# A bilinear graph layer on one core: weight sums on GpSimd, first words copied to PSUM, product 3 formed like the others, and a new order

## The chip, the cores and the metric

The kernel runs on one core of a Trainium2 chip. The metric is the device time of one execution in microseconds. The core has TensorE (PE, with its weight loads listed apart as PEld), VectorE (DVE), ScalarE (ACT), GpSimd (POOL) and SyncE (SP), which here issues the transfers. Engines work side by side and wait for each other on semaphores.

## The reference, cut to what matters

```
h   = relu(layernorm(x))                           # x: 64 batches of 256 x 768, fp32
ctx = (adj  @ (h @ Wadj.T)) / deg                  # adj: 64 x 256 x 256, 0 or 1
    + (adj' @ (h @ Wrev.T)) / rdeg
    +  h @ Wself.T                                 # three 768 x 768 weights
out = x + ctx + (a small term from the 0/1 relations through Wr, Wrr)
```

Biases are zero in the inputs. The work is in the three 768 x 768 products per batch and in the two products with adj.

## The kernel before, in words

**Words.** TensorE's fast fp32 form (fp32r) doesn't keep full precision, so each operand is split into words: `word0` is the value scaled by `LOWER` and written as fp32r by ScalarE, `rest` is the value less word0 (DVE), `word2` is the rest scaled by `STEP` (ACT), and `word1` is a combination of word0 and rest (DVE). One product of a weight sum and a left operand takes 12 matmuls of 128x384.

**Products.** A bilinear scheme takes 15 products of sums of weight blocks (a "right", a sum of 256x768 thirds of the weights, loaded as `raw`) with sums of thirds of the normalized input (a "left", from `h`). They run in two sweeps over the batches: sweep 1 does products 10, 5, 2, 8, 11, 14, 3, 13 for batches 1 to 62, sweep 2 does 9, 6, 7, 15, 12, 4, 1 for the same batches and the products with adj (`agg`). Intermediates `c` go to DRAM after sweep 1 and come back in sweep 2. Batches 0 and 63 are done by `whole` with plain fp32 matmuls straight from the raw blocks (72 in program order each, two instructions apiece in the trace): batch 0 in the opening, while the words of sweep 1 are made, and batch 63 in the changeover between the sweeps, while those of sweep 2 are made.

**Where the rights come from.** `prepare(n, s, rank)` makes the words of product n. Before, the sums of raw blocks are DVE `tensor_tensor` (L539), except product 3, whose name stands in `ON_PE`: TensorE forms its sum by multiplying the raw blocks with identity and minus-identity matrices (L502, fp32), and its rest and word 1 with scaled diagonals (L507, fp32r), all inside one PSUM buffer. Words come from ACT (L551 word0, L561 word2; L516 and L521 for product 3) and DVE (L555 rest, L565 word1; L526 casts for product 3). L555 and L565 read two SBUF operands.

**What orders the work.** Every operation is recorded in a `Plan` with an engine, an estimated duration and a rank; the table `OFFSETS` is added to ranks by the kind of operation. `Plan.schedule` then lists them: each engine takes the ready operation of the lowest rank, as long as buffers of its class are free (`SLOTS`, among them 4 PSUM buffers of class Q), and an operation with `lock` waits until the other locked one (DVE sums, rest and word1, and everything on POOL) is over by the estimates. What comes out is a fixed program order for each engine.

**The rest of a batch.** x is loaded, its statistics are taken on DVE (L714 to L724), the mean and scale go through DRAM and come back as a row over all partitions (`d`, then `row`, L729 and L736), POOL centres h (L745), DVE scales and clips it (L749). POOL adds thirds (L590), ACT and DVE make the left words (L600, L607, L613, L617), TensorE multiplies (L628), ACT scales a product between its two halves (L666) and DVE or ACT reads it (L676, L685, L687). In sweep 2 a small product `rows` with `token` (L638, tiles of 32 rows) is added.

Of the kernel before, what the change touches and what calls it, by code (L numbers as in the profile page):

```python
# [10 lines left out]
F32 = mybir.dt.float32  # L11
# [6 lines left out]
P = 128  # L18
# [62 lines left out]
ON_PE = (3,)  # L81
APART = (14,)
AHEAD = 5.0
PACE = 5.0
# [26 lines left out]
    "degree@": 18.6, "degree@1": -76.25, "diagonal": 16.77, "eT": -64.36, "eps": -1.93, "eps$": 8.55,  # L111
# [1169 lines left out]
```

## Time and profile before

| | |
|---|---|
| median of 3 runs | 2477.93 us (2477.17 to 2478.81) |
| profiled execution | 2478.37 us |
| its span in the profile | 2476.5 us (1.87 us lie around it) |
| PE busy | 2449.1 us, 99% |
| DVE, ACT, POOL busy | 85%, 72%, 52% |
| granted TensorE clock | 0.999 of full (2.4 GHz) |

Busy time counts overlapping records of pipelined matmuls once; the pitch between starts of matmuls tells what one costs. A line such as `[0.42 <-DVE x L793]` says that the engine sat idle for 0.42 us before this instruction, and which instruction ended last before it could go on.

### The profile page before, as it was taken

The numbers are of one execution on the slowest core, as the hardware profiler recorded it, in microseconds if no ns is written. First come the engines' busy times: TensorE is split into PE (matmuls) and PEld (weight loads), VectorE is DVE, ScalarE is ACT, GpSimd is POOL, SyncE is SP. The second block draws the span as 40 slices with busy tenths as digits, with TensorE's granted clock in tenths as the row PEclk, the third lists the DMA queues.
The fourth block names the chain that finished last, engine by engine and source line by source line (L and its number), as shares of the span: only waits on it lengthen the run. The fifth ranks groups of instructions, "written<-read, shape, count | busy, mean of one in ns | idle before, by whom it ended". The sixth has DMA issues, their size and how long they took to land.

```text
span 2476.5 us, 43288 instructions
## 1 busy us (share of the span) xinstructions
PE 2449.1 (99%) x13858; PEld 2365.0 (95%) x13858; DVE 2096.0 (85%) x4003; ACT 1777.2 (72%) x3772; POOL 1283.1 (52%) x1138
## 2 busy tenths in 40 slices
PE   6999999999999999999999999999999999999998
PEld 4899999999999999996999999999999999999998
DVE  7887888788788878878988889888888888888987
ACT  4788888888888888886666666666666666666665
POOL 1555555555555555543555555555555555555554
PEclk9999999999999999999999999999999999999999
DMA  5677777777777777876666666666666666666664
GB/s 214 241 284 281 268 277 284 271 274 282 277 268 280 285 270 275 293 254 215 223 214 216 216 217 212 216 217 215 213 213 213 216 215 216 217 216 214 215 219 135
DMA packets 224776, 590.66 MB, mean 239 GB/s; under 512 B 25080, under 2 KB 25080, under 8 KB 224544
## 3 DMA queue, kind: packets, MB, share of 16 engines
q1 hardware_dynamic: 224544, 587.86, 69.5%
q8 instruction: 110, 1.80, 0.3%
q14 instruction: 122, 1.00, 0.1%
HBM read 364.28 MB, written 223.48 MB: 237 GB/s over the span
## 4 chain that ended last, share of the span: by engine, by line
PE 97%; DVE 1%; DMA 1%; ACT 1%; issue 0%; POOL 0%; SPq 0%; ACTq 0%; POOLq 0%
PE x L628 21%; PE y L628 21%; PE agg L944 14%; PE z L628 10%; PE w L628 10%; PE t L628 5%; PE v L628 5%; PE u L628 5%; PE whole L782 2%; PE v L638 1%; DMA raw<-in_Wself_dram 0%; PE right L502 0%; PE pt L915 0%; DMA row<-d 0%; DVE right L555 0%
## 5 line engine op out<-in xcount | busy, mean ns | idle before, releaser
L932 POOL TENSOR_TENSOR hl<-c,hl 128x768 fp32r<-128x768 f32 x256 | 474.7, 1855 | 646.3 <-ACT hl L928 470.6
L628 PE MATMUL x<-word,left 128*128 128x384 f32 x2976 | 589.3, 339 | 0.2 <-DVE c L687 0.2
L628 PE MATMUL y<-word,left 128*128 128x384 f32 x2976 | 569.3, 335 | 0.0
L628 PEld LDWEIGHTS x<-word,left 128*128 128x128 f32 x2976 | 515.2, 188 | 14.2 <-issue 11.0
L628 PEld LDWEIGHTS y<-word,left 128*128 128x128 f32 x2976 | 517.8, 188 | 5.2 <-ACT y L666 1.0
L944 PE MATMUL agg<-hl,a 128*128 128x384 f32 x2048 | 395.3, 334 | 0.0
L944 PEld LDWEIGHTS agg<-hl,a 128*128 128x128 f32 x2048 | 358.4, 188 | 0.6 <-issue 0.2
L745 POOL TENSOR_TENSOR h<-h,row 128x768 f32<-128x768 f32 x128 | 234.6, 1855 | 177.5 <-DMA row<-d 132.2
L628 PE MATMUL z<-word,left 128*128 128x384 f32 x1488 | 299.3, 335 | 0.7 <-DVE x L793 0.4
L628 PE MATMUL w<-word,left 128*128 128x384 f32 x1488 | 298.2, 334 | 0.2 <-ACT w L666 0.2
L666 ACT ACTIVATE x<-x 128x768 f32<-128x768 f32 x248 | 191.8, 794 | 137.1 <-PE x L628 136.4
L628 PEld LDWEIGHTS z<-word,left 128*128 128x128 f32 x1488 | 258.7, 188 | 4.5 <-DVE x L793 0.7
L628 PEld LDWEIGHTS w<-word,left 128*128 128x128 f32 x1488 | 261.3, 188 | 0.8 <-ACT w L666 0.5
L955 DVE SCALAR_TENSOR_TENSOR c<-agg,rd,c 128x768 f32<-128x768 f32 x252 | 255.2, 1013 | 7.1 <-PE agg L944 3.9
L928 ACT ACTIVATE hl<-c 128x768 fp32r<-128x768 f32 x256 | 215.2, 841 | 30.9 <-DVE c L685 25.0
L666 ACT ACTIVATE y<-y 128x768 f32<-128x768 f32 x248 | 197.1, 795 | 41.5 <-PE y L628 41.4
L722 POOL TENSOR_TENSOR cols<-cols,half 128x2 f32<-128x2 f32 x64 | 83.0, 1296 | 252.7 <-DVE cols L721 252.7
L617 DVE SCALAR_TENSOR_TENSOR left<-left,top 128x256 fp32r<-128x256 f32 x496 | 199.5, 413 | 6.4
L685 DVE TENSOR_TENSOR c<-c,v 128x768 f32<-128x768 f32 x124 | 117.5, 947 | 102.0 <-PE v L628 101.1
L617 DVE SCALAR_TENSOR_TENSOR left<-left 128x256 fp32r<-128x256 f32 x434 | 203.3, 490 | 0.1
L607 ACT ACTIVATE top<-left 128x256 f32<-128x256 f32 x496 | 181.0, 383 | 6.2 <-DVE left L617 2.0
L676 ACT ACTIVATE c<-y 128x768 f32<-128x768 f32 x124 | 101.1, 815 | 70.0 <-PE y L628 69.9
(136 smaller groups left out, 4308.3 us busy)
## 6 DMA issues: line engine op xcount, KB each, us to landing
c<-kept SPq DMA_DIRECT2D x316, 384.0 KB
kept<-c SPq DMA_DIRECT2D x252, 384.0 KB
x<-in_x_dram SPq DMA_DIRECT2D x128, 384.0 KB
h<-in_x_t_dram SPq DMA_DIRECT2D x128, 384.0 KB
out_dram<-c SPq DMA_DIRECT2D x126, 384.0 KB
kept_h<-h SPq DMA_DIRECT2D x124, 384.0 KB
h<-kept_h SPq DMA_DIRECT2D x124, 384.0 KB
adj<-in_adj_dram SPq DMA_DIRECT2D x64, 512.0 KB
```

The lines of the kernel that those rows point to most:

```text
L607: lambda: nc.scalar.activation(view(top), t(w)[:, 0].bitcast(F32), AF.Copy),
L617: lambda: nc.vector.scalar_tensor_tensor(t(w)[:, 2], t(w)[:, 1].bitcast(F32), -STEP, first(), op0=ALU.mult, op1=ALU.add), s == 1,
L628: nc.tensor.matmul(t(q)[:, half, : H // 2], t(w)[:, lw, f, :], t(r[rw])[:, f, ts(half, H // 2)], start=start and i == 0 and f == 0, stop=s ...
L666: lambda: nc.scalar.activation(view(), view(), AF.Copy, scale=scale),
L676: lambda o=o, sign=sign: nc.scalar.activation(t(o).rearrange("p (k n) -> p k n", k=2), view(), AF.Copy, scale=sign * (1.0 if value_last el ...
L685: emit = lambda to=to, op=op: nc.vector.tensor_tensor(to(), to(), view(), op=op)
L722: pool(0.7, r - 21.5, f"pow {b}", [col], [col], lambda: nc.gpsimd.tensor_tensor(var(), var(), v["half"], op=ALU.pow))
L745: lambda h=h, one=one: nc.gpsimd.tensor_tensor(t(h), t(h), one(0), op=ALU.subtract),
L928: lambda: nc.scalar.activation(t(pair)[:, 0], t(o), AF.Copy, scale=LOWER),
L932: lambda: nc.gpsimd.tensor_tensor(t(pair)[:, 1], t(o), t(pair)[:, 0].bitcast(F32), op=ALU.subtract),
L944: nc.tensor.matmul(t(q)[:, half, : H // 2], t(s["a"])[:, c, k, ts(ic, P)], t(pairs[c])[:, part, ts(half, H // 2)], start=(c == 0 and part ...
L955: lambda q=q, to=to, ic=ic: nc.vector.scalar_tensor_tensor(to(), t(q)[:, :, : H // 2], t(rd)[:, ic, k : k + 1], to(), op0=ALU.mult, op1=AL ...
```

## The change

1. Product 3 is formed like the others: `ON_PE`, the diagonals and the whole branch of `prepare` for it are gone.
2. Sums of raw blocks move from DVE to POOL `tensor_tensor` (L488).
3. After word0, ACT copies it into a PSUM buffer of class Q (L507); rest (L511) and word1 (L521) read this copy, so each has one PSUM operand, and they are no longer locked against POOL.
4. The PSUM buffer held back for product 3's sums can serve as a Q buffer in the opening too.
5. `schedule` widens its look-ahead when nothing else can go on, and `OFFSETS` is a new table, so the order of all engines is new.

```diff
-ON_PE = (3,)
 OFFSETS = {
-    "a0+a1+b0+b1": 8.69, "a0+a1+b0+b1$1": -94.46, "a0+a1+b0+b1@1": -28.72, "a0+a2": 6.59, "a0+a2$1": 6.18,
...
-                    if e != "PE" and steps and o.rank > steps[-1].rank + PACE:
+                    if e != "PE" and steps and o.rank > steps[-1].rank + pace:
...
+            if not events and pace < 1000.0:
+                pace *= 2.0
+                continue
+            pace = PACE
...
-        if n in ON_PE:
-            minus, small = diagonal(s, -1.0, rank - 6.0), diagonal(s, -1.0 / STEP, rank - 6.0)
...
-                                nc.tensor.matmul(
-                                    view(), one, r[f][1]()[:, ts(h, H // 2)], start=i == 0, stop=i == len(parts) - 1
-                                )
...
-            return
...
-                    dve(
-                        on_dve(H), rank - 3.0 + 0.1 * f, f"right{n}", reads, [h],
-                        lambda h=h, f=f, r=r, op=op, src=src: nc.vector.tensor_tensor(t(h), src(), r[f][1](), op=op), True,
-                    )
...
+                pool(
+                    on_pool(H), rank - 3.0 + 0.1 * f, f"right{n}", reads, [h],
+                    lambda h=h, f=f, r=r, op=op, src=src: nc.gpsimd.tensor_tensor(t(h), src(), r[f][1](), op=op),
+                )
...
+            q = plan.buf("Q", [P, 2, 512], F32, f"copy{n}_{f}")
...
+            act(
+                in_place(H), rank - 1.8 + 0.1 * f, f"copy of {n}", [(w[0], f)], [q],
+                lambda f=f, view=view: nc.scalar.activation(view(), two(t(w[0])[:, f, :].bitcast(F32)), AF.Copy),
+            )
             dve(
-                on_dve(H), rank - 1.5 + 0.1 * f, f"rest of {n}", reads + [(w[0], f)], [h],
-                lambda f=f, h=h, src=src: nc.vector.scalar_tensor_tensor(
-                    t(h), src(), sign, t(w[0])[:, f, :].bitcast(F32), op0=ALU.mult, op1=ALU.subtract
-                ), True,
+                on_dve(H), rank - 1.5 + 0.1 * f, f"rest of {n}", reads + [q], [h],
+                lambda h=h, src=src, view=view: nc.vector.scalar_tensor_tensor(
+                    two(t(h)), two(src()), sign, view(), op0=ALU.mult, op1=ALU.subtract
+                ),
             )
```

By engine, sums go from 26 on DVE (16 in the opening) to 30 on POOL (20 in the opening); rest and word1 from 28 to 30 each; ACT gains 30 copies; TensorE loses 20 matmuls in program order, all in the opening.

TensorE in the opening, before (`whole` is batch 0 of plain fp32 matmuls, `right` is product 3's sum in PSUM):

```order
2 L782 MATMUL whole_0_647<-raw_0_607,h_0_605 128x384 x4
3 L502 MATMUL right_00_675<-raw_0_639,ident 128x384
4 L502 MATMUL right_00_675<-raw_0_641,diagonal-1.0_0_652 128x384
5 L502 MATMUL right_00_675<-raw_0_634,diagonal-1.0_0_652 128x384
6 L502 MATMUL right_01_687<-raw_0_639,ident 128x384
7 L502 MATMUL right_01_687<-raw_0_641,diagonal-1.0_0_652 128x384
8 L502 MATMUL right_01_687<-raw_0_634,diagonal-1.0_0_652 128x384
9 L782 MATMUL whole_0_647<-raw_0_644,h_0_605 128x384 x4
10 L782 MATMUL whole_0_711<-raw_0_641,h_0_636 128x384 x4
11 L507 MATMUL right_00_675<-word_0_718,diagonal-1.0_0_652 128x384
```

and of the change, at the end of the same stretch:

```order
14 L738 MATMUL whole_0_832<-raw_0_709,h_0_605 128x384 x4
15 L738 MATMUL whole_0_874<-raw_0_726,h_0_609 128x384 x4
16 L738 MATMUL whole_0_832<-raw_0_728,h_0_605 128x384 x4
17 L738 MATMUL whole_0_874<-raw_0_709,h_0_609 128x384 x4
18 L738 MATMUL whole_0_874<-raw_0_728,h_0_609 128x384 x4
19 L584 MATMUL y_1_968<-word_0_641,left_1_952 128x384 x4
20 L584 MATMUL y_1_968<-word_2_670,left_1_952 128x384 x4
```

The `whole` matmuls now follow each other without anything between them, and the first product (y of batch 1) comes right behind.

GpSimd in the opening, before (h is centred, then thirds of it are added):

```order
10 L745 TENSOR_TENSOR h_0_605<-h_0_605,row_628 128x768
11 L745 TENSOR_TENSOR h_0_636<-h_0_636,row_628 128x768
12 L722 TENSOR_TENSOR cols_89<-cols_89,half 128x2
13 L722 TENSOR_TENSOR cols_88<-cols_88,half 128x2
14 L745 TENSOR_TENSOR h_1_716<-h_1_716,row_849 128x768
15 L745 TENSOR_TENSOR h_1_694<-h_1_694,row_849 128x768
16 L590 TENSOR_TENSOR b2-a_0_1_929<-h_1_694,h_1_716 128x256
17 L590 TENSOR_TENSOR b0+b_0_1_934<-h_1_694 128x256
```

and of the change, from the 19th of the 20 sums on:

```order
31 L488 TENSOR_TENSOR right_0_849<-right_0_849,raw_0_713 128x768
32 L488 TENSOR_TENSOR right_1_861<-right_1_861,raw_0_713 128x768
33 L678 TENSOR_TENSOR cols_88<-cols_88,half 128x2
34 L701 TENSOR_TENSOR h_1_792<-h_1_792,row_841 128x768
35 L701 TENSOR_TENSOR h_1_827<-h_1_827,row_841 128x768
36 L546 TENSOR_TENSOR b2-a_0_1_938<-h_1_827,h_1_792 128x256
37 L546 TENSOR_TENSOR b0+b_0_1_941<-h_1_827 128x256
```

The 20 sums stand between the centring of batch 0 and that of batch 1.

TensorE in a period of sweep 2, before (batch 15; `rows` is the small product with tiles of 32 rows):

```order
2028 L944 MATMUL agg_14_17897<-hl_14_17781,a_17557 128x384 x4
2029 L944 MATMUL agg_14_17897<-hl_14_17858,a_17557 128x384 x4
2030 L638 MATMUL v_15_17828<-rows,token_91 128x384 x2
2031 L638 MATMUL u_15_17840<-rows,token_91 128x384 x2
2032 L628 MATMUL x_15_17738<-word_0_14161,left_15_17789 128x384 x4
2033 L628 MATMUL x_15_17738<-word_2_14175,left_15_17789 128x384 x4
```

and of the change:

```order
2008 L900 MATMUL agg_14_17935<-hl_14_17797,a_17590 128x384 x4
2009 L900 MATMUL agg_14_17935<-hl_14_17898,a_17590 128x384 x4
2010 L584 MATMUL x_15_17779<-word_0_14279,left_15_17818 128x384 x4
2011 L584 MATMUL x_15_17779<-word_2_14575,left_15_17818 128x384 x4
2012 L594 MATMUL v_15_17867<-rows,token_91 128x384 x2
2013 L594 MATMUL u_15_17880<-rows,token_91 128x384 x2
```

The four matmuls with `rows` moved behind eight of x, in each of the 62 periods.

## Rows read from the trace of the kernel before

**Rows 1.** Windows: stretch, us; then busy (x instructions) of each engine; clock, DMA, GB/s.

```profile
20.00:40.00 20.00, 20.00 (x61) 11.90 (x61) 18.13 (x22) 8.86 (x13) 1.41 (x1) 1.00 0.90 350
200.00:1020.00 820.00, 820.00 (x4722) 815.71 (x4721) 662.42 (x1477) 691.59 (x1379) 455.69 (x443) 1.00 0.77 277
1140.00:1180.00 40.00, 38.78 (x161) 27.42 (x160) 37.82 (x51) 22.39 (x49) 16.71 (x14) 1.00 0.52 189
1300.00:2400.00 1100.00, 1100.00 (x6392) 1075.13 (x6391) 977.06 (x1691) 710.97 (x1634) 578.57 (x477) 1.00 0.67 215
```

**Rows 2.** Timeline of PE in the opening: start, us, engine, line, operation.

```profile
18.93 7.20 PE L782 MATMUL whole<-raw,h 128*128 128x384 f32 x16 [18.93 <-DVE h L749]
...
26.61 1.45 PE L502 MATMUL right<-raw,diagonal-1.0_0_652 128*128 128x384 f32 x4
27.90 0.81 PE L502 MATMUL right<-raw,ident 128*128 128x384 f32 x2
...
76.09 2.16 PE L628 MATMUL y<-word,left 128*128 128x384 f32 x8
78.67 1.66 PE L628 MATMUL z<-word,left 128*128 128x384 f32 x8 [0.42 <-DVE x L793]
80.17 1.55 PE L628 MATMUL w<-word,left 128*128 128x384 f32 x8
81.56 0.68 PE L628 MATMUL y<-word,left 128*128 128x384 f32 x3
```

**Rows 3.** Groups of PE by line, 18 to 77 us: busy us, mean ns.

```profile
L502 PE MATMUL right<-raw,diagonal-1.0_0_652 128*128 128x384 f32 x16 | 5.8, 486 | 0.0
L502 PE MATMUL right<-raw,ident 128*128 128x384 f32 x8 | 3.2, 486 | 0.0
L507 PE MATMUL right<-word,diagonal-1.0_0_652 128*128 128x384 f32 x4 | 2.1, 556 | 0.0
```

**Rows 4.** Timeline of the start: issue of row, first centring on POOL.

```profile
11.26 0.35 SPq L736 DMA_DIRECT2D row<-d  x1
...
16.09 1.80 POOL L745 TENSOR_TENSOR h<-h,row 128x768 f32<-128x768 f32 x1 [8.95 <-DMA row<-d]
```

**Rows 5.** Groups of POOL: L932, L590 whole run; L745, L722 from 0 to 77 us.

```profile
L932 POOL TENSOR_TENSOR hl<-c,hl 128x768 fp32r<-128x768 f32 x256 | 474.7, 1855 | 646.3 <-ACT hl L928 470.6 <-DMA c<-in_x_dram 158.7 <-PE x L628 9.7
L745 POOL TENSOR_TENSOR h<-h,row 128x768 f32<-128x768 f32 x4 | 8.1, 2034 | 10.5 <-DMA row<-d 8.9 <-DMA h<-in_x_t_dram 1.5
L722 POOL TENSOR_TENSOR cols<-cols,half 128x2 f32<-128x2 f32 x3 | 3.4, 1120 | 39.5 <-DVE cols L721 39.5
...
L590 POOL TENSOR_TENSOR b0+b<-h 128x256 f32<-128x256 f32 x62 | 47.6, 768 | 4.5 <-DVE h L749 3.8 <-DVE line L724 0.7
```

**Rows 6.** Groups of ACT: L551 from 0 to 77 us; L666, L607 whole run.

```profile
L551 ACT ACTIVATE word<-right 128x768 fp32r<-128x768 f32 x10 | 8.1, 839 | 16.8 <-DVE right L539 16.6 <-PE whole L782 0.2
L666 ACT ACTIVATE x<-x 128x768 f32<-128x768 f32 x248 | 191.8, 794 | 137.1 <-PE x L628 136.4 <-DVE left L617 0.6
L607 ACT ACTIVATE top<-left 128x256 f32<-128x256 f32 x496 | 181.0, 383 | 6.2 <-DVE left L617 2.0 <-ACT left L600 0.3
```

**Rows 7.** DVE: sums in the opening; the read of a PSUM operand, whole run.

```profile
L539 DVE TENSOR_TENSOR right<-raw,raw 128x768 f32<-128x768 f32 x10 | 9.2, 952 | 0.2 <-DMA raw<-in_Wrev_dram 0.2
...
L685 DVE TENSOR_TENSOR c<-c,u 128x768 f32<-128x768 f32 x124 | 117.8, 950 | 0.3 <-PE u L628 0.2
```

**Rows 8.** Timeline: POOL and DVE side by side in the opening.

```profile
58.40 4.29 POOL L745 TENSOR_TENSOR h<-h,row 128x768 f32<-128x768 f32 x2
...
58.60 4.90 DVE L565 SCALAR_TENSOR_TENSOR word<-word,right 128x768 fp32r<-128x768 f32 x2
```

**Rows 9.** Waits of PEld, whole run: us in total, times, longest.

```profile
PEld v L638 <- DVE c L685: 15.0, 60, 0.3
```

**Rows 10.** Timeline of PEld: the small product in the first period of sweep 2 and in a later one.

```profile
1188.34 0.18 PEld L638 LDWEIGHTS v<-rows,token 32*128 32x128 f32 x2 [0.25 <-issue]
...
1518.19 0.18 PEld L638 LDWEIGHTS v<-rows,token 32*128 32x128 f32 x2 [0.25 <-DVE c L685]
```

More of the change, by code (lines that the diff above doesn't have):

```diff
@@ L326, in schedule @@
                 heapq.heappush(ready[o.eng], (o.rank, o.i, o))
-        events, done, now, locked, queue, out = [], 0, 0.0, 0.0, 0.0, []
+        events, done, now, locked, queue, out, pace = [], 0, 0.0, 0.0, 0.0, [], PACE
         steps = sorted((o for o in self.ops if o.eng == "PE"), key=lambda o: o.rank)[::-1]
@@ L477, in load_raw @@
         return raws[kn, s]
-    diagonals = {}
-    def diagonal(s, scale, rank):
-        if (s, scale) not in diagonals:
-            d = diagonals[s, scale] = plan.buf("S", [P, P], F32R, f"diagonal{scale}_{s}")
-            act(0.3, rank, "diagonal", [], [d], lambda: nc.scalar.activation(t(d), v["ident"], AF.Copy, scale=scale))
-        return diagonals[s, scale]
     def prepare(n, s, rank):
@@ L490, in prepare @@
         w = words[n] = [plan.buf("W", [P, 2, H], F32R, f"word{n}_{i}") for i in range(3)]
-        if n in ON_PE:
-            minus, small = diagonal(s, -1.0, rank - 6.0), diagonal(s, -1.0 / STEP, rank - 6.0)
-            for f in range(2):
-                for h in range(2):
-                    q = plan.buf("U", None, None, f"right{n}_{f}{h}", inside=hold)
-                    view = lambda q=q: t(q)[:, : H // 2]
-                    part = lambda a, f=f, h=h: t(a)[:, f, ts(h, H // 2)]
-                    def total(view=view, f=f, h=h):
-                        for i, (sign, r) in enumerate(parts):
-                            one = v["ident"] if sign == "+" else t(minus).bitcast(F32)
-                            nc.tensor.matmul(
-                                view(), one, r[f][1]()[:, ts(h, H // 2)], start=i == 0, stop=i == len(parts) - 1
-                            )
-                    def take(d, view=view, part=part):
-                        nc.tensor.matmul(view(), t(d), part(w[0]), start=False, stop=True, skip_group_check=True)
-                    at = rank + 0.2 * f + 0.1 * h
-                    key = (f, h)
-                    pe(
-                        0.17 + 0.65 * len(parts), at - 3.0, f"right of {n}", [r[f][0] for _, r in parts] + [minus], [q], total
-                    )
-                    act(
-                        in_place(H // 2), at - 2.0, f"word0 of {n}", [q], [(w[0], key)],
-                        lambda view=view, part=part: nc.scalar.activation(part(w[0]), view(), AF.Copy, scale=LOWER),
-                    )
-                    pe(0.35, at - 1.5, f"rest of {n}", [minus, (w[0], key), q], [q], lambda take=take: take(minus))
-                    act(
-                        in_place(H // 2), at - 1.0, f"word2 of {n}", [q], [(w[2], key)],
-                        lambda view=view, part=part: nc.scalar.activation(part(w[2]), view(), AF.Copy, scale=STEP),
-                    )
-                    pe(0.35, at - 0.5, f"less of {n}", [small, (w[0], key), q], [q], lambda take=take: take(small))
-                    dve(
-                        on_dve(H // 2), at - 0.3, f"word1 of {n}", [q], [(w[1], key)],
-                        lambda view=view, part=part: nc.vector.tensor_copy(part(w[1]), view()),
-                    )
-            return
@@ L531, in prepare @@
             h = halves[f]
-            if len(parts) > 1:
-                for i, (sign, r) in enumerate(parts[1:]):
-                    src = parts[0][1][f][1] if i == 0 else (lambda h=h: t(h))
-                    reads = [parts[0][1][f][0], r[f][0]] if i == 0 else [h, r[f][0]]
-                    op = ALU.add if sign == "+" else ALU.subtract
-                    dve(
-                        on_dve(H), rank - 3.0 + 0.1 * f, f"right{n}", reads, [h],
-                        lambda h=h, f=f, r=r, op=op, src=src: nc.vector.tensor_tensor(t(h), src(), r[f][1](), op=op), True,
-                    )
-                assert parts[0][0] == "+"
-        sign = -1.0 if parts[0][0] == "-" and len(parts) == 1 else 1.0
+            for i, (sign, r) in enumerate(parts[1:]):
+                src = parts[0][1][f][1] if i == 0 else (lambda h=h: t(h))
+                reads = [parts[0][1][f][0], r[f][0]] if i == 0 else [h, r[f][0]]
+                op = ALU.add if sign == "+" else ALU.subtract
+                pool(
+                    on_pool(H), rank - 3.0 + 0.1 * f, f"right{n}", reads, [h],
+                    lambda h=h, f=f, r=r, op=op, src=src: nc.gpsimd.tensor_tensor(t(h), src(), r[f][1](), op=op),
+                )
+        assert parts[0][0] == "+" or len(parts) == 1
+        sign = -1.0 if parts[0][0] == "-" else 1.0
         for f in range(2):
             h = halves[f]
+            q = plan.buf("Q", [P, 2, 512], F32, f"copy{n}_{f}")
+            two = lambda a: a.rearrange("p (k n) -> p k n", k=2)
+            view = lambda q=q: t(q)[:, :, : H // 2]
             if len(parts) > 1:
@@ L1084, in main_path @@
         psum = main.enter_context(tc.tile_pool(name="psum", bufs=1, space=bass.MemoryType.PSUM))
-        singles = ExitStack()
-        single = singles.enter_context(tc.tile_pool(name="single", bufs=1, space=bass.MemoryType.PSUM))
-        held, late = None, None
+        now, turns = ExitStack(), ["early", "single", "late"]
+        single = now.enter_context(tc.tile_pool(name=turns[0], bufs=1, space=bass.MemoryType.PSUM))
         plan = Plan(SLOTS)
@@ L1104, in main_path @@
         record(nc, plan, fixed, B, NREL)
-        for o in plan.schedule():
+        order = plan.schedule()
+        held = next(b.slot for b in plan.bufs if b.name == "hold")
+        for o in order:
             for b in o.bufs:
-                if b.name == "hold":
-                    held = b.slot
-                elif b.tile is None:
+                if b.tile is None and b.name != "hold":
                     home = {"Q": psum, "U": single, "S": small}.get(b.cls, pool)
-                    if b.cls == "Q" and b.slot == held:
-                        if late is None:
-                            singles.close()
-                            late = main.enter_context(tc.tile_pool(name="late", bufs=1, space=bass.MemoryType.PSUM))
-                        home = late
+                    if b.cls == "U" or b.cls == "Q" and b.slot == held:
+                        if (b.cls == "U") != (turns[0] == "single"):
+                            now.close()
+                            del turns[0]
+                            single = now.enter_context(tc.tile_pool(name=turns[0], bufs=1, space=bass.MemoryType.PSUM))
+                        home = single
                     b.tile = home.tile(b.shape, b.dtype, tag=f"{b.cls}{b.slot}", name=b.name)
             o.emit()
+        main.push(now)
     def general_path(sub: ExitStack):
```

22 lines of the change are left out of this document (11 added, 11 removed), and 278 rows, old and new, of the table OFFSETS.

## The prediction, made before the change was run

> **What bounds the kernel now.** I read the windows first, to see in which stages TensorE is not full [rows 1]. From 200 to 1020 us (sweep 1) and from 1300 to 2400 us (sweep 2) it is busy for all 820 and all 1100 us, with VectorE, ScalarE and GpSimd below it. In these stages only fewer or better packed matmuls can save time, and the change takes none away there. What is left is the opening, where TensorE doesn't start before 18.93 us and then works on batch 0 [rows 2], a short wait of 0.42 us at 78.67 [rows 2], and the changeover, with 1.2 us of idle PE between 1140 and 1180 us [rows 1]. So I read the timeline of PE in the opening next. The reader is to see that it is full from 18.93 to 76.09 us, that what fills it are `whole` and the 32 matmuls of product 3's sums, and that what ends its first wait is the normalized h, behind the row that comes back from DRAM at 16.09 us [rows 4].
>
> The sums are made against the profiled execution: 2478.37 us, 0.44 us above the median of 2477.93 us.
>
> **The change, part by part.**
>
> *TensorE loses product 3's sums.* 24 fp32 instructions (L502) and 8 fp32r ones (L507, four as in the row and four with the other diagonal) [rows 3]. Their means of 486 and 556 ns overlap, so I take pitches: four fp32 in 27.90 − 26.61 = 1.29 us, 0.3225 each; eight fp32r in 81.56 − 80.17 = 1.39 us, 0.174 each [rows 2]. 24 × 0.3225 + 8 × 0.174 = 7.74 + 1.39 = 9.1 us. From the other side: `whole` alone would be 7.04 us for its first 16 (from 18.93 to the first L502, which stood six pitches ahead of 27.90, at 25.97) plus 128 × 0.3225 = 41.3 us, and 57.16 − 48.3 = 8.8 us. I take 9.0, with 8.8 and 9.1 as bounds. `whole` would then end near 18.9 + 48.2 = 67.1 us.
>
> *Whether anything else is ready by 67.1 us* decides how much of this counts. The first y needs the words of product 5, made long before, and left words of batch 1, which stand behind 20 weight sums on GpSimd. The trace has no such sum on POOL. The nearest row is a 128x768 tensor_tensor with two SBUF inputs, 1855 ns over 256 in the whole run; in the opening the same form took 2034 ns [rows 5], but there it overlapped VectorE instructions that read two SBUF operands: two of L745 took 4.29 us just where two of L565 took 4.90 [rows 8]. With the copy in PSUM, L511 and L521 become like L685, whose 950 ns show no such stretching beside POOL [rows 7]. So I take 1855. The chain: centring batch 0 from 16.09, two at 1.8 to 19.7; 20 × 1.855 = 37.1, to 56.8; two pows (L722, 1.12 each) to 59.0; centring batch 1, 3.7, to 62.7; two thirds at 0.77, to 64.2; then the left words, two steps on ACT and two on DVE of the same 256 columns, each near L607's 383 ns [rows 6] and a hand-over, to about 65.9. That is 1.2 us before 67.1. The end of `whole` still decides, but narrowly.
>
> *ScalarE.* 16 copies to PSUM come in the opening. A 768-wide copy into PSUM isn't in the trace; bounds are 794 ns in place in PSUM (L666) and 839 ns from SBUF to SBUF (L551) [rows 6]. I take 0.8: 12.8 us more, less about 1.1 from product 3's parts and the diagonals. ACT was busy only 8.86 us of the 20 between 20 and 40 us [rows 1], so together 48 word instructions of about 0.8 = 38 us lie in the 46 us between 20 and 66, behind POOL's pace of one sum per 1.855 us. Hidden by `whole`; without that cover the excess over POOL's chain would show.
>
> *VectorE* loses 16 sums of 952 ns [rows 7] and four casts, and gains four instructions of about 0.95: 11 to 13 us less. It was on no path of PE but for short waits, so I count nothing for it.
>
> *The late products.* Before, the first products lost 0.42 us waiting for x [rows 2]. After, the second half of the first y waits for a scale on ACT that stands behind the copies of product 14, which themselves need a PSUM buffer that `whole` leaves late; two copies and a scale at 0.8 are 2.4 us, against 1.4 to 2.8 us of other matmuls (8 to 16 at 0.174). I count nothing, and ±1.5 us.
>
> *The start.* In SP's list one raw load (768 KB) ahead of d and row is replaced by an h (384 KB). At the 350 GB/s that the queues moved at [rows 1] 384 KB are 1.1 us. If row isn't held up by that load nothing changes. 0 to 1.1; I take 0.5.
>
> *The changeover.* Ten sums move to POOL (18.6 us at 1855), and POOL was busy 16.71 of the 40 us from 1140 on [rows 1]. PE stood idle for 1.2 us; the new order puts eight matmuls of v ahead of batch 63's last products. I take 1.0 us back, between 1.5 lost (if POOL's hl, needed by agg, comes late) and 1.5 gained.
>
> *The sweeps.* In sweep 1 the second half of product 13 moves four matmuls forward; every scale that a second half waits for keeps at least eight matmuls (1.39 us) of cover against 0.79 of a scale. In sweep 2 product 4's second half has eight instead of twelve. The moved `rows` matmuls had the largest named wait, 15.0 us over 60 periods on a DVE read [rows 9], and eight more matmuls would cover that read. But the first period shows the same 0.25 us with "issue" as its end [rows 10]: the gap is there without the DVE wait. So I count 0 for it. By the Trainium skill, page "TensorEngine Tiling (Array Packing)", section "Key Properties", changing the tiling mode drains TensorE, which fits a gap at both entries to 32-row tiles; by that rule too the sum gets nothing.
>
> Sum: 2478.4 − 9.0 − 0.5 − 1.0 = 2467.9, so **2468 us**, with its own range of 2465.5 to 2470.5 from the bounds above.
>
> **The rivals.**
>
> *A, GpSimd becomes the bound of the opening.* At the opening's own 2034 ns [rows 5] the 20 sums take 3.6 us more, the left words come at 69.5 and the first y waits 2.4 us: 2470.3. At 2145 ns, half of the 4.29 [rows 8], 5.8 us more and 4.6 us of wait: 2472.5. For it: the margin is only 1.2 us, and raw blocks may land late. Against: the PSUM copies. The Trainium skill, "GPSIMD Engine Reference", section "Engine selection", speaks against the move: elementwise work on a tile belongs on VectorE, GpSimd being about twice as slow with two inputs. The trace agrees on the ratio, 1855 against 952 ns; by the rule alone VectorE should keep the sums. That costs only where POOL ends last, which is this rival.
>
> *B, a new wait in every period of a sweep* (the other side). Product 4's scale in sweep 2 has 1.39 us for about 0.2 of waiting for the matmul's end, 0.79 of scaling and 0.1 or so to be seen: 0.3 to spare. If ACT comes to it later by more than that, for example because a left word ahead of it in ACT's list waits for a DVE read, each 0.1 us costs 62 × 0.1 = 6.2 us. From 0.17 us a period on, the gain of 10.5 is gone; at 0.25 the time is 2468 + 15.5 = 2483.4, slower. Against it: ACT is busy 711 of 1100 us in sweep 2 [rows 1], so a late ACT isn't the rule.
>
> *C, the DVE wait of `rows` is real.* If PE loses about 0.09 us a period of the 0.25 (the matmul ahead of it covers the rest), 62 × 0.09 = 5.6 us more come back: 2462.3. Rows 10 speak against it.
>
> *D, the changeover turns worse.* Hl and the sums queue on POOL, and a raw block comes late: 2 to 5 us lost instead of 1.0 gained: 2471 to 2474.
>
> **How the numbers follow.** Chances: forecast 0.62, A 0.14, B 0.09 (half of it beyond no change), C 0.07, D 0.08. The range from 2462.5 to 2473.5 holds the forecast, A, C nearly, and most of D, and leaves out about 0.15. Faster by over 0.2% (5.0 us, about what a measurement of this kernel can tell from no change) means below 2473.0: the forecast, A, C, most of D and a little of B, 0.88. Within 0.2%: 0.08. Slower: 0.04.
>
> **What would show it.** In the changed profile the `whole` group should run from 18 to 19 us for 48 us without a break, the first y should start at 66.5 to 68 with little idle before it, and L488 should read about 1.86 us. The windows of both sweeps should hold as many matmuls as before, give or take one in a thousand. If L488 reads 2.0 or more and y names POOL or the left words as what it waited for, A is right. If the wait of `rows` falls and the period with it, C is. If a wait of PE for ACT's t shows 60 times, B is. The prediction is wrong altogether if the opening shortens by 9 us and the sweeps lose it, or if the left words come well after 67 us.

## The result, and the profile after

The changed kernel takes 2503.56 us (median; 2500.62 to 2504.39) against 2478.37 us for the kernel before: ratio 1.01, 95% interval 1.0082 to 1.0117. It is **slower**, by about 25 us or 1.0%, where 10.5 us of gain were forecast. The profiled execution takes 2500.62 us, with a span of 2498.8 us and a granted clock of 0.999.

First the opening. The timeline of PE in the changed kernel answers to [rows 2]:

```profile
19.57 48.86 PE L738 MATMUL whole<-raw,h 128*128 128x384 f32 x144 [19.57 <-DVE h L705]
68.41 1.93 PE L584 MATMUL y<-word,left 128*128 128x384 f32 x8
72.54 0.96 PE L584 MATMUL y<-word,left 128*128 128x384 f32 x4 [2.20 <-ACT y L622]
73.54 1.66 PE L584 MATMUL z<-word,left 128*128 128x384 f32 x8
...
81.42 0.76 PE L584 MATMUL w<-word,left 128*128 128x384 f32 x3 [0.68 <-DVE cols L677]
```

`whole` runs as one block, and the first y comes at 68.41 instead of 76.09: 7.7 us ahead. Then TensorE waits 2.20 us for the first y's scale and 0.68 us at 81.42. The windows answer to [rows 1]:

```profile
20.00:40.00 20.00, 20.00 (x57) 11.51 (x57) 12.53 (x14) 12.20 (x16) 20.00 (x12) 1.00 0.89 340
200.00:1020.00 820.00, 820.00 (x4722) 815.64 (x4721) 657.02 (x1473) 692.60 (x1380) 455.68 (x444) 1.00 0.80 278
1140.00:1180.00 40.00, 38.67 (x172) 29.00 (x171) 35.77 (x49) 27.69 (x55) 25.93 (x21) 1.00 0.51 172
1300.00:2400.00 1100.00, 1091.43 (x6278) 1054.38 (x6278) 998.30 (x1661) 702.98 (x1609) 593.09 (x468) 1.00 0.66 211
```

Sweep 1 holds 4722 matmul records in 820 us, as before. Sweep 2 holds 6278 in 1100 us where it held 6392, at the same clock. 114 matmuls at the 0.174 us of [rows 2] are 19.8 us of work that didn't fit into these 1100 us. So the loss is in sweep 2.

The small product with `rows` stands once in each of its periods. Before, its first start is at 1188.34 [rows 10] and its last at 2456.06: 1267.7 us. After, they are at 1183.70 and 2477.03: 1293.3 us. The distances between two starts (periods, from here on) were all 20.81 to 20.85 us before, but for the first and the last. After, there are two kinds among the 61: 30 are 20.82 or 20.83, and 23 are 21.65 to 22.16, typically 21.77. The other eight are the first, the last three and four of 20.91 to 21.30. The ledger of the profiled executions: 4.6 us ahead at 1183.70, 25.6 lost between the first and the last `rows`, and the rest, 1.3, behind the last one: 22.3 us, the difference of 2500.62 and 2478.37.

The waits of the changed kernel name one release in sweep 2 which the kernel before doesn't show for PE, and for PEld once, with 0.2 us:

```profile
PEld x L584 <- DVE c L641: 17.5, 26, 0.7
...
PE x L584 <- DVE c L641: 9.1, 23, 0.4
```

Why VectorE is late is seen in the timeline of the changed kernel, by setting a short period (from 1208) beside a long one (from 1229). L573 is the second step of a left word (product 6's and 7's here, both operands in SBUF), L888 GpSimd's subtraction for the lower word of c, L641 the reads of TensorE's results:

```profile
1208.15 0.75 DVE L573 SCALAR_TENSOR_TENSOR left<-left 128x256 fp32r<-128x256 f32 x2
1208.59 2.02 POOL L888 TENSOR_TENSOR hl<-c,hl 128x768 fp32r<-128x768 f32 x1 [1.60 <-ACT hl L884]
1208.82 1.81 DVE L641 TENSOR_TENSOR c<-c,t 128x768 f32<-128x768 f32 x2
...
1229.41 2.13 POOL L888 TENSOR_TENSOR hl<-c,hl 128x768 fp32r<-128x768 f32 x1 [1.74 <-ACT hl L884]
1229.42 2.41 DVE L573 SCALAR_TENSOR_TENSOR left<-left 128x256 fp32r<-128x256 f32 x2
1231.75 1.81 DVE L641 TENSOR_TENSOR c<-c,t 128x768 f32<-128x768 f32 x2
...
1234.74 0.94 DVE L641 TENSOR_TENSOR c<-c,x 128x768 f32<-128x768 f32 x1
...
1235.73 0.97 PE L584 MATMUL x<-word,left 128*128 128x384 f32 x4 [0.40 <-DVE c L641]
```

The same two instructions take 0.75 us where GpSimd starts 0.44 us behind them, and 2.41 us where it starts 0.01 us ahead. Of the 2.41 the pair's first instruction takes 0.42 and its second 2.07, to 0.29 us behind the end of GpSimd's, which itself takes 2.13 instead of the 1.855 of [rows 5]. So by these times GpSimd's instruction came in between the two. The reads of t and x come 1.66 us later, and TensorE, whose next product is added to the buffer of x, waits for the second of them. Over sweep 2, 23 such pairs took 2.39 to 2.43 us; in 22 of them GpSimd had started 0.01 to 0.03 us ahead, in the last one 0.07 us behind. Where it started within a microsecond behind a pair that took 0.75, it was 0.44 us behind or more, 34 times. 21 of the 23 long periods hold a long pair, and the other two long pairs stand in the last periods. The two long periods without one have causes of their own: in that of 22.16 L888 holds the instruction ahead of the pair (L569, 2.09 us instead of 0.42), and in that of 21.65 ACT comes late, which is told below.

This agrees with the Trainium skill, page "SBUF — State Buffer", section "SBUF: two separate sides": of a VectorE operation with two SBUF inputs and a GpSimd operation that reads SBUF, whichever starts first holds the shared ports for its whole instruction. The rows show the hold over a whole instruction, 2.07 us against 0.42. Which of the two comes first isn't to be read from the recorded starts alone: with GpSimd's 0.01 us ahead, the pair's first instruction still ran in 0.42 us.

The timeline also shows what brings the two together. About 4.5 us earlier in the period VectorE makes another such pair, of products 1 and 9, and GpSimd adds two thirds (b1+b) for product 15. These rows are from the same short period and the same long one:

```profile
1203.83 0.76 DVE L573 SCALAR_TENSOR_TENSOR left<-left 128x256 fp32r<-128x256 f32 x2
1204.33 0.85 POOL L546 TENSOR_TENSOR b1+b<-h 128x256 f32<-128x256 f32 x1 [0.60 <-DVE left L573]
...
1224.66 1.30 DVE L573 SCALAR_TENSOR_TENSOR left<-left 128x256 fp32r<-128x256 f32 x2
1224.87 0.81 POOL L546 TENSOR_TENSOR b1+b<-h 128x256 f32<-128x256 f32 x1 [0.30 <-DVE c L641]
```

Where the addition starts 0.04 to 0.29 us behind the start of this first pair, the pair takes 1.30 us; where it starts 0.33 us behind or later, 0.75. VectorE then reaches the second pair 4.76 us behind the first instead of 4.31, and L888 starts 4.75 us behind the first in both periods: so they meet. In sweep 2 the first pair is lengthened in 25 periods, and 23 of these hold a long second pair; no other period does. When the addition starts is set by a load of h from DRAM: in 56 of 59 periods it starts 0.16 us behind the landing of a transfer that it waits for. The groups of GpSimd in sweep 2, in the changed kernel and in the one before, show that this wait is new:

```profile
L546 POOL TENSOR_TENSOR b1+b<-h 128x256 f32<-128x256 f32 x60 | 49.6, 827 | 41.4 <-DMA h<-kept_h 22.0 <-DVE left L573 7.7 <-DVE c L641 5.2
...
L590 POOL TENSOR_TENSOR b1+b<-h 128x256 f32<-128x256 f32 x60 | 44.6, 743 | 1.4 <-DMA h<-kept_h 1.0 <-DVE left L613 0.4
```

No run moved this load, so the step from it to the first pair is read from the timelines and not tested.

Before, a pair of this kind stood elsewhere. In its timeline, L932 is GpSimd's subtraction and L617 the second step of the left words:

```profile
1522.29 1.85 POOL L932 TENSOR_TENSOR hl<-c,hl 128x768 fp32r<-128x768 f32 x1 [1.46 <-ACT hl L928]
1522.64 0.94 DVE L685 TENSOR_TENSOR c<-c,v 128x768 f32<-128x768 f32 x1
1523.50 0.94 DVE L685 TENSOR_TENSOR c<-c,x 128x768 f32<-128x768 f32 x1
...
1524.37 0.76 DVE L617 SCALAR_TENSOR_TENSOR left<-left 128x256 fp32r<-128x256 f32 x1
```

Beside GpSimd's subtraction VectorE read PSUM; the left words came when it was over. The one shown met the addition behind it instead (0.76 us against 0.41), and the periods stayed at 20.8 us.

### The profile page after: what moved, and what is told of

The parts are those of the page before. It is cut to its first block, busy times and chain, and to the rows that moved or that the text cites. A ratio compares the mean times of both kernels' runs of the same rounds, so it can differ in the third digit from the quotient of the medians.

```text
span 2498.8 us, 43744 instructions
## 1 busy us (share of the span) xinstructions
PE 2455.0 (98%) x13826; PEld 2356.6 (94%) x13826; DVE 2119.7 (85%) x3977; ACT 1804.2 (72%) x3796; POOL 1359.8 (54%) x1168
## 3 DMA queue, kind: packets, MB, share of 16 engines
q8 instruction: 111, 1.82, 0.3%
## 4 chain that ended last, share of the span: by engine, by line
PE 93%; DVE 4%; DMA 1%; ACT 1%; issue 1%; POOL 0%; DVEq 0%; SPq 0%; ACTq 0%; POOLq 0%
PE x L584 21%; PE y L584 20%; PE agg L900 13%; PE w L584 10%; PE z L584 10%; PE v L584 5%; PE t L584 5%; PE u L584 5%; PE whole L738 3%; DVE c L911 1%; DVE c L641 1%; PE v L594 1%; DVE h L705 0%; DMA raw<-in_Wadj_dram 0%; DVE left L569 0%
## 5 line engine op out<-in xcount | busy, mean ns | idle before, releaser
L888 POOL TENSOR_TENSOR hl<-c,hl 128x768 fp32r<-128x768 f32 x256 | 486.7, 1902 | 390.0 <-ACT hl L884 218.5
L584 PEld LDWEIGHTS x<-word,left 128*128 128x128 f32 x2976 | 516.8, 188 | 20.5 <-DVE c L641 17.5
L900 PE MATMUL agg<-hl,a 128*128 128x384 f32 x2048 | 405.5, 339 | 1.1 <-DVE c L641 0.4
L622 ACT ACTIVATE x<-x 128x768 f32<-128x768 f32 x248 | 197.4, 796 | 187.2 <-PE x L584 181.1
L573 DVE SCALAR_TENSOR_TENSOR left<-left 128x256 fp32r<-128x256 f32 x434 | 229.8, 553 | 0.1
L573 DVE SCALAR_TENSOR_TENSOR left<-left,top 128x256 fp32r<-128x256 f32 x496 | 195.3, 414 | 6.3
L641 DVE TENSOR_TENSOR c<-c,v 128x768 f32<-128x768 f32 x124 | 118.3, 954 | 69.9 <-PE v L584 41.4
L546 POOL TENSOR_TENSOR a1+a<-h 128x256 f32<-128x256 f32 x62 | 49.3, 794 | 195.6 <-DMA h<-kept_h 128.4
```

What stands on the lines that cost most here:

```text
L573: lambda: nc.vector.scalar_tensor_tensor(t(w)[:, 2], t(w)[:, 1].bitcast(F32), -STEP, first(), op0=ALU.mult, op1=ALU.add), s == 1,
L584: nc.tensor.matmul(t(q)[:, half, : H // 2], t(w)[:, lw, f, :], t(r[rw])[:, f, ts(half, H // 2)], start=start and i == 0 and f == 0, stop=s ...
L622: lambda: nc.scalar.activation(view(), view(), AF.Copy, scale=scale),
L641: emit = lambda to=to, op=op: nc.vector.tensor_tensor(to(), to(), view(), op=op)
L888: lambda: nc.gpsimd.tensor_tensor(t(pair)[:, 1], t(o), t(pair)[:, 0].bitcast(F32), op=ALU.subtract),
L900: nc.tensor.matmul(t(q)[:, half, : H // 2], t(s["a"])[:, c, k, ts(ic, P)], t(pairs[c])[:, part, ts(half, H // 2)], start=(c == 0 and part ...
```

## The experiments

Theory 1: the loss is the collision of the pair L573 with L888 in sweep 2, which the new order of VectorE made possible. Theory 2, the rival: the pair is only where the lateness shows, and the new order of the other engines (the moved `rows` of TensorE, the other places on ACT and SyncE) or the state in which the opening leaves sweep 2 makes it; then moving the pair changes little. All kernels are the changed one with the edit shown; times of before beside them were 2478.9 to 2479.4 us.

### e1_pair_later

```diff
         order = plan.schedule()
+        for b in range(4, B - 4):
+            for n in (6, 7):
+                order = shift(order, f"left2 {n} {b}", f"read 4 {b - 1}")
```

`shift` puts the named operation behind the other in the list; only VectorE's order changes.

> The changed kernel with one thing moved: in the periods of batches 4 to 59 of sweep 2, VectorE makes the third left words of products 6 and 7 behind its two reads of t instead of ahead of them; TensorE, ScalarE, GpSimd and SyncE keep their order. Theory 1 (VectorE and GpSimd collide on SBUF: where GpSimd's subtraction for hl starts a few hundredths of a us ahead of this pair, the pair takes 2.41 us instead of 0.75, and the period 21.77 instead of 20.82): the long periods go from 56 of 62 places, and 0.9 x 24 = 22 us come back, so about 2479 us. Theory 2 (the new order of sweep 2 leaves VectorE too little room, or h and c come late from DRAM, and the pair only shows it): the long periods stay, 2498 to 2505 us.

Measured: 2484.08 us (2481.18 to 2487.33, 10 runs), 1.0023 times before (1.0013 to 1.0033). 19 of the 25 us are back. The timeline, at the same place of a period:

```profile
1522.42 1.85 POOL L898 TENSOR_TENSOR hl<-c,hl 128x768 fp32r<-128x768 f32 x1 [1.74 <-ACT hl L894]
1522.64 1.82 DVE L651 TENSOR_TENSOR c<-c,t 128x768 f32<-128x768 f32 x2
1524.38 0.75 DVE L583 SCALAR_TENSOR_TENSOR left<-left 128x256 fp32r<-128x256 f32 x2
```

The reads of PSUM run beside GpSimd at full pace (1.82 for two), and the pair behind it takes 0.75. The first pair of the period is still lengthened to 1.30 us in 24 periods of 20.83, so that meeting alone costs no time. Periods are 20.82 to 20.94 again, but for five of 21.01 to 21.51 and for the last batches, where the pair wasn't moved (21.69, 24.94 and 18.49 stand where before had 20.85, 20.84 and 21.35). Theory 1 holds for the bulk of the loss. From the first to the last `rows` 5.4 us more than before are left: 1.4 in the first period, 2.0 in the odd ones, 2.1 at the end.

### e2_sweep2_of_before

Entries of `OFFSETS` for most kinds of sweep 2 were set to those of before, two of them shown:

```diff
-"left2 6": -12.15
+"left2 6": -257.52
...
-"left2 7": -195.54
+"left2 7": -271.35
```

> The changed kernel with the old table's entries for the operations of sweep 2, so that TensorE, VectorE and GpSimd run sweep 2 in the order of before; opening, sweep 1 and changeover as in the change. If the loss lies in the order of sweep 2 (theories 1 and 2): sweep 2 takes as long as before, and what is left is the lead of 4.6 us that the change has when sweep 2 begins: 2474 us. Rival (the loss comes with the sums, the copies or the buffers, whatever the order): still above 2490 us.

Measured: 2524.65 us (2522.36 to 2526.41), 1.0189 times before: a miss. The orders of ACT and SyncE came out as a mixture of the two kernels, and TensorE waited for ACT's scale of x, which it does in neither of the two, as the waits show:

```profile
PE x L585 <- ACT x L623: 22.7, 31, 1.6
```

So it says nothing about the order of before. This mixed order costs 46 us; which of ACT's rows held the scale wasn't followed up.

### e3_no_copy and e4_sums_on_vector

These take one part of the change back in the opening and keep the order. In e3 the 30 copies to PSUM are gone, and rest and word 1 read word 0 in SBUF; in e4 the sums are on VectorE.

```diff
-                lambda f=f, view=view: nc.scalar.activation(view(), two(t(w[0])[:, f, :].bitcast(F32)), AF.Copy),
+                lambda: None,
...
-                    lambda h=h, f=f, r=r, op=op, src=src: nc.gpsimd.tensor_tensor(t(h), src(), r[f][1](), op=op),
+                    lambda h=h, f=f, r=r, op=op, src=src: nc.vector.tensor_tensor(t(h), src(), r[f][1](), op=op),
```

> The changed kernel with the same order, but without the copies of word0 into PSUM: rest and word1 read word0 from SBUF, so both their operands lie there. If GpSimd's sums and such VectorE instructions shut each other out, the 32 of them in the opening and the 20 sums take turns: a sum and two of them take 1.85 + 2 x 0.95 = 3.7 us instead of 1.9, the left words come late, and the first y starts at 80 us or later instead of 68.4. Rival (the copies buy nothing): the first y stays within 1 us of 68.4, and the 2.2 us wait behind it shrinks, since ScalarE has 12.8 us less to do.

> The changed kernel with its 30 weight sums on VectorE instead of GpSimd, everything else as it is. VectorE was busy 28.5 of the 40 us from 20 to 60; 20 sums of 0.95 are 19 us more. If VectorE then is the bound: the first y starts 4 to 8 us later than 68.4. Rival (there is room, since sums of 0.95 instead of 2.0 us make everything behind them earlier): the first y stays within 1 us of 68.4, and the move to GpSimd isn't what the opening's gain rests on.

Measured: 2534.25 us without the copies, 2519.54 us with the sums on VectorE (one run each). Without copies the first y waits 17.96 us for its left words and starts at 85.92 instead of 68.41. The groups of this opening show why:

```profile
L488 POOL TENSOR_TENSOR right<-raw,raw 128x768 f32<-128x768 f32 x12 | 29.4, 2472 | 0.6 <-DMA raw<-in_Wadj_dram 0.6
L521 DVE SCALAR_TENSOR_TENSOR word<-word,right 128x768 fp32r<-128x768 f32 x14 | 29.2, 2092 | 0.2
```

With two SBUF operands word 1 takes 2092 ns instead of the 951 of the changed kernel, and the sums beside it 2472 instead of 1896. In this order the copies are worth 17.5 us. With the sums on VectorE the timeline of PE reads:

```profile
53.14 15.72 PE L738 MATMUL whole<-raw,h 128*128 128x384 f32 x48 [1.03 <-ACT c L755]
72.89 2.93 PE L584 MATMUL y<-word,left 128*128 128x384 f32 x8 [4.02 <-ACT left L556]
```

4.5 us later than with them on GpSimd. Both parts do what the change wants of them in the opening. The rest of both losses lies mostly in the changeover, where ten sums and their words are made in the same way: the first `rows` of sweep 2 starts at 1213.17 in e3 and at 1197.03 in e4, against 1183.70. The long periods of sweep 2 stand in both.

### e5_sweep2_all_of_before

As e2, but for all kinds of sweep 2, so that all five engines have the steady order of before there. Opening, sweep 1 and changeover stay as in the change.

> As in the earlier run with sweep 2's old entries, but with all of them: in that run ScalarE and SyncE had kept a mixture of both tables' orders, and TensorE waited 20 us for ScalarE's scaled x. Now all five engines run a period of sweep 2 in the order of before, and opening, sweep 1 and changeover in the order of the change. Theory 1 (collisions of VectorE and GpSimd that the new order of sweep 2 brings): no long periods, 2478.4 minus the lead of 4 to 5 us: 2474 us. Rival (something else of the change, such as where buffers lie, makes sweep 2 longer): long periods remain, above 2480 us.

Measured: 2488.46 us (2487.9 to 2491.86), 1.0038 times before (1.0024 to 1.0052). In the middle of sweep 2 all periods are 20.80 to 20.95 us, none long: theory 1 again. But the first three `rows` distances are 21.52, 24.47 and 18.99 and the last three 22.58, 25.12 and 21.99, where before had 17.38 and two of 20.8, and 20.85, 20.84 and 21.35. The first and the last batches have entries of their own in the table, and these were still the new ones: 12.6 us at the seams between two orders.

### e6_mended, e7_h_later, e8_y_later

The opening's waits: e7 loads the second half of batch 0's h behind the row's fetch, so that GpSimd's second centring doesn't hold VectorE's first scaling. e8 moves the second half of the first y behind z and w, and its scale ahead of product 14's copies. e6 is e5 with both.

```diff
+        order = shift(order, "xt0 0", "row 0")
...
+        order = shift(order, "second 5 1", "first 11 1")
+        order = shift(order, "scale 5 1", "copy of 14", True)
```

> The changed kernel with the second load of h moved behind the fetch of row. If the first scaling of h on VectorE (2.6 us from 16.96 to 19.57) is held up by the second centring on GpSimd: TensorE starts at 18.0 us instead of 19.6, with perhaps a wait of up to 1 us where the second h comes in. Rival (held up by something else): it starts at 19.5 us again.

> The changed kernel with the second half of the first y moved behind the first halves of z and w, and its scale ahead of product 14's copies on ScalarE. If the wait of 2.2 us is the place in the order alone: no wait over 0.3 us in the first 8 us of products, and TensorE is 2 us ahead by 80 us. Rival (the left words or product 14's words are late, and the next matmul inherits the wait): 1 to 2 us of waits appear at z, w or the next y.

> The same, with two things moved in the opening: the second load of h behind the fetch of row (so that GpSimd's second centring doesn't start right where VectorE's first scaling of h wants SBUF), and the second half of the first y behind the first halves of z and w, with its scale ahead of product 14's copies. If both waits are what they look like: 1.5 us at the start and 1.8 us behind the first y, so 2470.5 us. Rival (GpSimd's chain to the left words sets the start of the products, so what is gained at the start is lost at the first y): 2473 to 2474 us.

Measured: e7 2499.11 us, e8 2506.96 us (one run each), e6 2495.22 us (2491.54 to 2495.86), 1.0057 times before. e6 is 6.8 us slower than e5. In e7 PE starts at 18.69, but the first y at 68.33, as without the edit; and 18.69 lies within the starts of runs without it (18.56 to 19.57), so no gain is shown. In e8 the wait doesn't go, it moves to z:

```profile
67.30 1.93 PE L594 MATMUL y<-word,left 128*128 128x384 f32 x8
73.87 2.90 PE L594 MATMUL z<-word,left 128*128 128x384 f32 x8 [4.64 <-DVE word L531]
```

z needs a PSUM buffer that a copy of word 0 holds until VectorE has formed word 1 from it. The copies' price is thus that they compete for the four Q buffers with the first products, which I hadn't costed.

### e9_sweep2_with_edges, e10_sweep2_and_ends, e11_old_tail

e9 takes the old table entries for the first and last batches of sweep 2 too; TensorE's order is then that of before from the second period of sweep 2 on, and nearly so in the first. e10 adds those of batches 0 and 63. e11 has the old ones for all but the first batch, so that the changeover stays new.

> The changed kernel, with the whole of sweep 2, its first and last batches included, in the order that it had before the change; opening, sweep 1 and changeover keep the new order. Theory 1 (the time was lost by VectorE pairs that GpSimd held in sweep 2, and by the edges of the last order in the two runs ahead): no period of sweep 2 longer than before the change, and what is left of the opening's gain counts, 4 to 5 us: about 2474 us. Rival (the opening's order arrives in another state at sweep 2, and the last batches lose time whatever their order): 2479 to 2485 us.

> As the run ahead, but with the old places for the batches that only end or only begin in sweep 2 as well. Theory 1: the same, about 2474 us. Rival: 2479 to 2485 us, or a difference between the two of more than 3 us, which would put the loss at the border of the sweeps.

> As e9, but the first batch of sweep 2 keeps the new places, so that the changeover runs in the new order up to the first product of sweep 2, and the last batches have the old places. Theory 1: the changeover then gives up nothing (first small product of sweep 2 near 1184 us, as in the changed kernel), every later period lasts 20.83 us but perhaps the first two or three, and the whole takes 2473 to 2476 us, faster than before the change. Rival (what e9 lost ahead of sweep 2 hangs on how the opening happened to run, not on the order of the first batch): 2478 to 2481 us, with the first small product at 1186 us or later.

Measured: e9 2479.62 us (2477.33 to 2482.19, 11 runs), 1.0002 times before (0.9993 to 1.0012); e10 2487.5 us, 1.0031 times (1.002 to 1.0043); e11 2482.22 us, 1.0012 times (1.0003 to 1.0021). e9's window in sweep 2 is that of before to one matmul:

```profile
1300.00:2400.00 1100.00, 1100.00 (x6393) 1074.91 (x6392) 978.61 (x1692) 711.30 (x1632) 578.37 (x476) 1.00 0.67 215
```

All its periods but the first and the last are 20.82 or 20.83, and from the first to the last `rows` it takes 1268.5 us (1267.7 before, 1293.3 in the change). So the loss of the changed kernel is shown to lie in the order of sweep 2 and in nothing that the opening leaves behind: theory 2's second half falls. But the time is that of before, not 5 us under it. `rows` first starts at 1186.75, 1.6 us ahead of before, where the changed kernel was 4.6 ahead; and 0.7 of the 1.6 are four matmuls of product 4 that now stand behind it. The timeline of PE in the changeover shows why:

```profile
1158.23 9.70 PE L740 MATMUL whole<-raw,h 128*128 128x384 f32 x24 [2.29 <-DVE c L913]
1167.86 0.45 PE L596 MATMUL rows<-rows,token 32*128 32x384 f32 x4
1168.83 1.65 PE L586 MATMUL x<-word,left 128*128 128x384 f32 x8 [0.52 <-ACT c L757]
...
1175.81 0.97 PE L586 MATMUL v<-word,left 128*128 128x384 f32 x4 [0.73 <-DVE left L571]
...
1181.69 1.66 PE L902 MATMUL agg<-hl,a 128*128 128x384 f32 x8 [0.74 <-DVE x L913]
```

These waits and one of 1.23 us ahead of them are 5.5 us, against 2.0 in the changed kernel's changeover, and `whole` takes 9.70 us here where it takes 8.01 there (the clock, below). In e10 the first `rows` starts at 1194.50, 6.2 us later than before, and from it to the last one 1267.6 us pass, as before: its whole loss lies ahead of sweep 2, at the border, as its expectation allowed for. e11, which keeps that changeover, loses at the first seam (periods of 21.53, 24.23, 18.96) and had a later opening. None of the versions tried beats the kernel before.

## Why the prediction was wrong

*TensorE loses product 3's sums*: right, if a little below its bounds. From the start of `whole` to the first y it takes 48.84 us instead of 57.16: 8.3 us back, where 9.0 were predicted, between 8.8 and 9.1. Over the runs with this opening the first y starts between 67.05 and 68.92.

*The chain on GpSimd*: right in its prices, and rival A didn't come, but the chain left out a link. In the opening's groups of the changed kernel the sums take 1.90 and 1.84 us, by 1.855 predicted, and the copies to PSUM 0.81 by 0.8:

```profile
L488 POOL TENSOR_TENSOR right<-raw,raw 128x768 f32<-128x768 f32 x12 | 22.3, 1896 | 0.6 <-DMA raw<-in_Wadj_dram 0.6
L488 POOL TENSOR_TENSOR right<-right,raw 128x768 f32<-128x768 f32 x8 | 14.5, 1837 | 0.0
...
L507 ACT ACTIVATE copy<-word 128x768 f32<-128x768 f32 x16 | 12.9, 808 | 0.4
```

ACT's first word of b0+b, which the first y needs, was ready at 68.35, where the prediction had the left words at 65.9. Between centring batch 1 and adding its thirds h is scaled on VectorE; the prediction counted nothing for that, and GpSimd waited 3.02 us for it. The timelines of GpSimd and of PE's weight loads:

```profile
66.42 0.73 POOL L546 TENSOR_TENSOR b2-a<-h,h 128x256 f32<-128x256 f32 x1 [3.02 <-DVE h L705]
...
68.41 0.65 PEld L584 LDWEIGHTS y<-word,left 128*128 128x128 f32 x4 [0.59 <-ACT left L556]
```

VectorE's statistics came 2.08 us late for GpSimd, too, but only one pow of 0.69 stood behind them, not two of 1.12. The margin of 1.2 us was gone. That it costs hardly a wait is luck: `whole` also ended later than the 67.1 predicted, its last matmul starting at 67.94, and the first y came 0.1 us later than the pitch allowed. e3 and e4 show what each protects: 17.5 and 4.5 us.

*The late products*: mis-sized. Counted at 0 ±1.5; measured 2.20 us for ACT's y, 0.68 and another 0.33 us at 99, less the 0.42 of before: 2.8 us. The sentence had the right place, the scale behind product 14's copies, and put too much cover over it; e8 shows that moving the scale only moves the wait.

*The start*: −0.5 predicted, +0.6 measured in this run. The row did come 1 us earlier, as the timeline of the changed kernel shows:

```profile
15.13 3.57 POOL L701 TENSOR_TENSOR h<-h,row 128x768 f32<-128x768 f32 x2 [7.68 <-DMA row<-d]
...
16.96 5.03 DVE L705 SCALAR_TENSOR_TENSOR h<-h,row 128x768 f32<-128x768 f32 x2 [9.27 <-POOL h L701]
```

But both halves of h were there by then, so GpSimd's second centring ran on without a pause to 18.70, and VectorE's first scaling, ready at 16.96, was over at 19.57 only. Before, GpSimd paused between the two [rows 4], and the scaling took 0.96 us from 17.92. It is the collision of sweep 2 in small. The start also varies by itself: PE starts between 18.56 and 19.57 us in the runs that have the changed order here.

*The changeover*: −1.0 predicted, about zero measured: 4.9 us ahead by 100 us (7.7 less 2.8), 4.6 at 1183.70.

*The sweeps*: this step failed. "So I count 0 for it" was reasoned from the cover of the scales and of the moved `rows` matmuls, that is from TensorE and ACT. It never asked where VectorE's left words with two SBUF operands now stand against GpSimd's `hl`, though [rows 8] had shown what such a meeting costs (4.29 and 4.90 us side by side) and the opening was reckoned with it. In sweep 2 the new order puts a pair of them 0.44 us ahead of where `hl` begins, and whenever VectorE is held by that much they meet. The 21 long periods with a long pair cost 0.95 us each, 19.9 of the 25.6 lost between the first and the last `rows`; the one with a long L569 1.3, the one with a late ACT 0.8, four odd periods (20.91 to 21.30) 1.1, and the first and the last three 1.4 and 1.2. The 1.3 us behind the last `rows` aren't traced. Sweep 1 has no such loss, 820 us for as many matmuls as before.

*Rival B* had the right kind, a new wait in many periods of sweep 2 that turns the gain into a loss, with 2483.4 us as its time, but another place. Its own place (a left word ahead of t's scale on ACT) is met, too: PE waits for ACT's t three times, 0.9 us in all, and in the period of 21.65 the row ahead of the scale is the left word, held by a transfer:

```profile
1504.05 0.42 ACT L556 ACTIVATE left<-a1+a 128x256 fp32r<-128x256 f32 x1 [2.64 <-DMA out_dram<-c]
1504.38 0.79 ACT L622 ACTIVATE t<-t 128x768 f32<-128x768 f32 x1
```

So B was right at this one place and had 0.8 us for it; the wait that decided was on VectorE, and I hadn't looked for it there.

*Rival C* stays refuted: in e9, with the old order, the wait of `rows` is again 15.0 us over 60 periods, and in the changed kernel PEld has 15.5 us over 62 with "issue" as its end. The 0.25 us of gap are there whichever wait is named:

```profile
PEld v L594 <- issue: 15.5, 62, 0.3
```

What stays open: why the load of h lands at another place in each period, and whether an earlier load alone would end the long periods; no run tried it. Nor was a kernel found with the changed opening and changeover and the old sweep 2 without a seam; the gain of 4.6 us is only shown to arrive at sweep 2, not to reach the end.

## What to carry to other kernels

When an order changes, list for each steady stage the VectorE instructions with two SBUF operands and the GpSimd instructions, and ask which of them can now start at the same moment; a full TensorE hides neither. A difference in matmul records per window (6278 against 6392) finds the stage of a loss, and the distances between one instruction's starts in successive periods tell a slow period from slow work. A table of ranks isn't taken over in part without a price: of six kernels that had part of the old one (e2, e5, e6, e9 to e11), one was level with before and five lost 3 to 46 us, mostly where two orders met.

## What the runs showed of the hardware

Two VectorE instructions with two SBUF operands, one right behind the other, take 0.75 us by themselves and 2.41 us where a GpSimd instruction of about 1.85 us comes in between. Whether one does hangs on tenths of a us: an addition that started 0.04 to 0.29 us behind the first of the two lengthened the pair, one that started 0.33 us behind or later didn't. So a kernel with one fixed order has two lengths of period, 20.83 and 21.77 us.

The granted clock after the same wait isn't the same in each run. Eight runs have the wait of 2.19 to 2.21 us ahead of the first y's second half; the clock stays at 1.00 behind it in five of them and falls to 0.50 in three (e5, e7, e11). In e11 TensorE stands still for 2.21 us ahead of 73.06; the windows from 71 to 79 us then read (the clock is the first number behind the last bracket):

```profile
71.00:73.00 2.00, 0.00 (x0) 0.00 (x0) 1.93 (x4) 1.93 (x5) 0.37 (x1) 1.00 1.01 383
73.00:75.00 2.00, 1.94 (x6) 1.94 (x7) 2.00 (x4) 1.69 (x4) 1.26 (x1) 0.51 0.85 255
75.00:77.00 2.00, 2.00 (x10) 2.00 (x9) 2.00 (x6) 1.23 (x4) 0.68 (x2) 0.63 0.99 390
77.00:79.00 2.00, 2.00 (x13) 2.00 (x12) 0.90 (x3) 2.00 (x4) 1.75 (x1) 1.00 0.20 78
```

That is the lower of the two levels, 1.2 GHz; four matmuls of y take 1.65 us there instead of the 0.96 of the changed kernel, whose clock stays at 1.00 after 2.20 us of the same wait. In e9's changeover the clock is 0.67 and then 0.50 in the four microseconds that follow its wait of 2.29 us, and `whole` takes 9.70 us for 24 matmuls instead of 8.01 in e11. So a wait of just over 2 us cost another 1.2 us in e11's opening (5.13 instead of 3.88 us from the start of y's second half to that of z's) and 1.7 us in e9's changeover.
